# A scan along the adjacency's rows in place of triangle products, in the first layer of a graph network

## The chip, the cores and the metric

The kernel runs on one core of one Trainium2 chip. The metric is the device time of one execution in microseconds (us). The profile is of one execution, taken by the hardware profiler.

The engines are called as the profile calls them: PE multiplies matrices, PEld is its loading of weights, DVE is the vector engine, ACT the scalar engine with its activation functions, POOL the general engine (GpSimd), and SP issues transfers. Each works through a fixed list of instructions in order and waits where an operand isn't ready.

## What is computed

Four graph layers run over 2708 nodes with 512 features, with one adjacency matrix of 2708 x 2708 zeros and ones (int32). Each layer ends with a residual and a layer norm. The change touches layer 0, and the mask that the later layers read:

```
Ab   = A > 0
keep = Ab & (cumsum(Ab, axis=1) <= 64)          # each node's first 64 neighbours
cnt  = keep.sum(axis=1)
xj   = leaky_relu((keep @ X) / max(cnt, 1) @ W_nb.T + b_nb)
xi   = leaky_relu(X @ W_line.T + b_line)
x    = layernorm(X + xi + where(cnt > 0, xj, 0))
# layer 1: mask = A > 0; agg = mask @ x / max(mask.sum(1), 1); ...
# layers 2 and 3: attention over A > 0
```

So layer 0 has to know, for each one in a row of A, whether it is among the first 64 of its row. Layer 1 and the attention layers need the whole mask.

## The kernel before, in words

Rows and columns are cut into NT = 22 tiles of 128 nodes, the last with 20. `maskT` is the transposed mask, kept on the chip for the whole program in 8-bit floats: `maskT[p, j, i]` belongs to neighbour 128 j + p and node i.

**Mask stage of layer 0** (the loop of lines 276 to 296). For each tile t PE makes two products of 512 x 512 weights with the transposed features: `pm0` with W_nb (line 280), which `keep_y` (214) splits into a high part yH (ACT) and a low part yL (DVE)[...]; and `pm1` with W_line (288), to which DVE adds the bias (290) and applies leaky (182), after which POOL adds the residual (292) and stores r0 to memory (293). Beside that `load_mask` (234, POOL's queue) brings 128 rows of A as bf16, `count` (240 to 245, DVE) counts each row's ones and derives four small columns (`iso`, `has`, `rkeep`, `rdeg`), and `turn` (249 to 259) transposes the rows with 22 small PE products into maskT, with ACT copying out. Mask tiles have two buffers `m`. Up to t = 2 the order on PE is written by hand (`pe`); later each engine's list follows from the program's order, its priorities and readiness as the scheduler sees them. `issue_after` lets `count` stand after a given instruction.

**Sums of layer 0** (393 to 421). The node tiles form six blocks (`cuts`): tiles 20 and 21 first, then five blocks of four. For each block the loop goes over the 22 neighbour tiles j; such a pass through the loop is called a step here. Two PE products per step keep a running count of neighbours in `cum` (a buffer of pm0): with `upper`, a triangle of ones, which gives the count down to each row of this tile (311), and with `below`, its complement, which completes the tile's count afterwards (401). DVE compares the running count with 64 and multiplies by the mask, which gives kT (313). kT has two buffers. Four or eight products (408) add kT times yH and yL to one sum per node tile. Beside it two generators step on: `todo`, which finishes the previous block's nodes (`finish`, 321: two steps for each node tile, with the layer norm and the store of x1), and `later`, which multiplies layer 1's weights together (`weights1`, 339) and forms vectors for the attention layers (`vectors`, 370). `later` steps once in block 1, from j = 2 in block 2, and every second time from there.

**Layer 1** makes its products per tile (426 to 436: yH, yL again, and z1), and then its sums (439 to 456), where ACT widens maskT to fp32 (447) and PE multiplies it with yH and yL (450).

The transfer queues: mask loads, r0, x1 and z1 stores are issued by POOL; feature rows, weights and read-backs by SP.

Of the kernel before, what the change touches and what calls it, by code (L numbers as in the profile page):

```python
# [30 lines left out]
def kernel(  # L31
# [43 lines left out]
    rkeep = const.tile([P, NT], F32, name="rkeep")  # L75
    for c, value in ((iso, 0.0), (has, 0.0), (rdeg, 1.0), (rkeep, 1.0)):
        nc.vector.memset(c, value)

    dcol = const.tile([P, NT, H], F32, name="dcol")
    nc.vector.memset(dcol, 0.0)  # L80


# [41 lines left out]

    def transpose_weight(pool, psum, dst, src):

        for ki in range(KD):
            wr = pool.tile([P, D], F32, name="wr", bufs=4)
            nc.sync.dma_start(wr, src[ki * P:(ki + 1) * P, :])
            ps = psum.tile([P, KD, P], F32, name="ps_tr")  # L130
            for ko in range(KD):
                pe(nc.tensor.transpose(ps[:, ko, :], wr[:, ko * P:(ko + 1) * P], ident))
            nc.vector.tensor_copy(dst[:, :, ki * P:(ki + 1) * P], ps)  # L133
# [47 lines left out]
    def leaky(dst, u):  # L181
        nc.vector.scalar_tensor_tensor(dst, u, 0.01, u, op0=OP.mult, op1=OP.max)

# [6 lines left out]
    with ExitStack() as phase:  # L190
        yp = phase.enter_context(tc.tile_pool(name="y", bufs=1))

        upper = yp.tile([P, P], BF16, name="upper")
        make_upper_triangular(nc, upper)
        below = yp.tile([P, P], BF16, name="below")
        nc.vector.tensor_scalar(below, upper, -1.0, 1.0, op0=OP.mult, op1=OP.add)
        weight2 = yp.tile([P, KD, D], F32, name="weight2")
# [20 lines left out]
        def product(xT, n, w, which, order=as_it_comes):  # L218
# [3 lines left out]
            return pm  # L222

        def rows_of(src):
            return early(2, NT, lambda t: fetched(src, t, rows(t)))

        with ExitStack() as ph:
            st = ph.enter_context(tc.tile_pool(name="l0a", bufs=2))
            wnT, wlT = weight(), weight2

            def load_mask(t):
                n = rows(t)
                m = st.tile([P, N], BF16, name="m")
                nc.gpsimd.dma_start(m[:n], adj[t * P:t * P + n, :], max_dma_last_dim=N * 2)
                return m

            def count(t, m):
                n = rows(t)
                cnt = sm.tile([P, 1], F32, name="cnt")
                nc.vector.tensor_scalar(m[:n], m[:n], 0.0, None, op0=OP.is_gt, op1=OP.add, accum_out=cnt[:n])  # L240
                one = slice(t, t + 1)
                nc.vector.tensor_scalar(iso[:n, one], cnt[:n], 0.0, None, op0=OP.is_equal)
                nc.vector.tensor_scalar(has[:n, one], cnt[:n], 0.0, None, op0=OP.is_gt)
                nc.vector.tensor_scalar(rkeep[:n, one], cnt[:n], KEEP, 1.0, op0=OP.min, op1=OP.max)
                nc.vector.tensor_scalar(rdeg[:n, one], cnt[:n], 1.0, None, op0=OP.max)

            def turn(t, m, order=as_it_comes):
                n = rows(t)
                for g0 in range(0, NT, G):
                    g1 = min(g0 + G, NT)  # L250
                    ps = sums(BF16, (P, G, P))
                    for j in range(g0, g1):
                        w = rows(j)
                        order(nc.tensor.transpose(ps[:w, j - g0, :n], m[:n, j * P:j * P + w], identb[:n, :n]))  # L254
                    parts = [(P, g0, min(g1, FULL))] + ([(rows(FULL), FULL, NT)] if g1 > FULL else [])
                    for w, a, b in parts:
                        if a < b:
                            nc.scalar.copy(maskT[:w, a:b, t * P:t * P + n], ps[:w, a - g0:b - g0, :n],
                                           saturate=False)

            xs = rows_of(x)
            xTs = early(0, NT, lambda t, order=as_it_comes: transposed(ahead, ps_tr, xs(t), rows(t), "xT", order))
            ms = {}

            transpose_weight(st, ps_tr, wnT, l0_w_nb)
            lows = {}
            for t in range(2):
                xT = xTs(t, order=pe)  # L270
                lows[t] = keep_y(t, P, product(xT, P, wnT, 0, pe))
            transpose_weight(st, ps_tr, wlT, l0_w_line)
            b_line = bias(bcast(l0_b_line, D))
            for i in range(2):
                ms[i] = load_mask(i)
            for t in range(NT):
                n = rows(t)
                order = pe if t < 3 else as_it_comes
                if t > 1:
                    lows[t] = keep_y(t, n, product(xTs(t), n, wnT, 0, order))  # L280
                xT = xTs(t)
                if t + 1 < NT:
                    xTs(t + 1)
                for q in range(0 if t == 2 else t - 1, t) if t > 1 else ():
                    turn(q, ms[q], order)
                    if q + 2 < NT:
                        ms[q + 2] = load_mask(q + 2)
                pm = product(xT, n, wlT, 1, order)
                u = sm.tile([P, D], F32, name="u")
                nc.vector.tensor_add(u[:n], pm[:n], b_line[:n])  # L290
                leaky(u[:n], u[:n])
                nc.gpsimd.tensor_add(u[:n], u[:n], xs(t))
                nc.gpsimd.dma_start(r0_dram[t * P:t * P + n, :], u[:n])
                with tc.issue_after(lows[t].ins):
                    count(t, ms[t])
            turn(NT - 1, ms[NT - 1])
            nc.vector.reciprocal(rkeep, rkeep)
            nc.vector.reciprocal(rdeg, rdeg)

        with ExitStack() as ph:
            st = ph.enter_context(tc.tile_pool(name="l0b", bufs=1))
            b_nb = bias(bcast(l0_b_nb, D))
            cuts = [(b, min(b + 4, NT)) for b in range(0, NT, 4)]
            cuts = cuts[-1:] + cuts[:-1]

            def kept(cum, b, j):
                cols, w = slice(b[0] * P, b[1] * P), (b[1] - b[0]) * P  # L310
                nc.tensor.matmul(cum[:, :w], upper, maskT[:, j, cols], start=(j == 0), stop=True, skip_group_check=True)  # L311
                kT = st.tile([P, 512], F32R, name="kT", bufs=2)
                nc.vector.scalar_tensor_tensor(kT[:, :w], cum[:, :w], KEEP, maskT[:, j, cols],  # L313
                                               op0=OP.is_le, op1=OP.mult)
                return kT

            def begin(b):
                cum = ps_mm.tile([P, D], F32, name="pm0")
                return cum, kept(cum, b, 0)

            def finish(ts_, us):
                for t in ts_:
                    n, u = rows(t), us[t]
                    r0 = fetched(r0_dram, t, n)
                    nc.vector.tensor_add(u[:n], u[:n], b_nb[:n])
                    leaky(u[:n], u[:n])
                    yield
                    nc.vector.scalar_tensor_tensor(u[:n], u[:n], has[:n, t:t + 1], r0, op0=OP.mult, op1=OP.add)
                    layer_norm(sm, u[:n], n, u[:n])
                    nc.gpsimd.dma_start(x1_dram[t * P:t * P + n, :], u[:n])  # L330
                    yield
# [60 lines left out]

            todo, later = iter(()), chain(weights1(), vectors())
            cum, kT = begin(cuts[0])
            for i, b in enumerate(cuts):
                ts_ = range(*b)
                cols, w = slice(b[0] * P, b[1] * P), (b[1] - b[0]) * P
                pa = {t: sums() for t in ts_}
                for j in range(NT):
                    if j + 1 < NT:  # L400
                        nc.tensor.matmul(cum[:, :w], below, maskT[:, j, cols], start=False, stop=True,  # L401
                                         skip_group_check=True)
                        nxt = kept(cum, b, j + 1)
                    elif i + 1 < len(cuts):
                        cum, nxt = begin(cuts[i + 1])
                    for t in ts_:
# [4 lines left out]
                    next(todo, None)  # L411
                    if i == 1 and j > 1 or i > 1 and j % 2 or i == 0 and j == 2:
                        next(later, None)
                us = {}
# [4 lines left out]
                todo = finish(ts_, us)  # L419
            for _ in later:  # L420
                pass
# [4 lines left out]
            for t in range(NT):  # L426
                n = rows(t)
                xT = xTs(t)
                keep_y(t, n, product(xT, n, wnb[0], 0))
                if t + 1 < NT:  # L430
                    xTs(t + 1)
# [794 lines left out]
```

## Time and profile before

| | us |
|---|---|
| three runs | 3123.17, 3125.3, 3129.33 |
| median | 3125.3 |
| profiled execution, span | 3125.8 |
| its PE busy | 3009.5 (96%) |
| its DVE busy | 1988.8 (64%) |
| its ACT busy | 1401.3 (45%) |

The span falls into the mask stage of layer 0 (to 218 us), the sums of layer 0 (218 to 537), the products of layer 1 (537 to 698), its sums (698 to 924) and the attention layers, over two thirds of the time. A line of a view names the place in the kernel (L408 is line 408), the engine, the operation, and the tile that is written and those that are read (`kT<-pm,maskT`). "Idle before <-" is time in which the engine had nothing to do ahead of these instructions, with what ended it. PE's ends are modelled because products are pipelined, so starts are the better measure: the distance of two starts is what an instruction costs.

### The profile page before, as it was taken

Reading aid. Unit: us, or ns where it says so; the run is one execution under the profiler, and the core shown is the slowest. Engines: PE = TensorE matmul, PEld = TensorE weight load, DVE = VectorE, ACT = ScalarE, POOL = GpSimd, SP = SyncE. Lnnn points to the kernel's source line nnn. Section 1 sums busy time; section 2 is a strip of 40 time slices with the busy share of each in tenths; the row PEclk is TensorE's granted clock in tenths of the full one; section 3 lists DMA queues with packets and bytes.
Section 4 is the critical chain, followed back from the end, with each engine's and each line's share of the span. In section 5 each row is a group of like instructions: output and inputs, shape, how many; then the busy total and the mean of one; then the engine's idle time right before and its main releaser. Section 6 shows DMA issues by size and latency. Waiting matters only on the chain.

```text
span 3125.8 us, 37086 instructions
## 1 busy us (share of the span) xinstructions
PE 3009.5 (96%) x14888; PEld 1647.0 (53%) x14888; DVE 1988.8 (64%) x2562; ACT 1401.3 (45%) x1575; POOL 223.2 (7%) x352
## 2 busy tenths in 40 slices
PE   8999999999999999999998999999999999999998
PEld 4556666448887433333356333333356455555555
DVE  5562765212233899999986999999963524345342
ACT  2431000112224688888863788899863000000011
POOL 2220010101110000000012000000000000000001
PEclk9999999999999999999999999999999999999999
DMA  5651421322222000110024010011021000000000
GB/s 137 139 127 35 121 64 41 108 65 81 81 70 76 15 29 35 39 44 30 28 80 145 22 39 28 27 38 33 20 97 48 4 14 17 24 14 22 14 19 21
DMA packets 114287, 163.31 MB, mean 52 GB/s; under 512 B 39494, under 2 KB 62311, under 8 KB 114104
## 3 DMA queue, kind: packets, MB, share of 16 engines
q1 hardware_dynamic: 88152, 109.21, 11.5%
q0 software_dynamic: 16064, 47.95, 5.6%
q10 hardware_dynamic: 9888, 3.67, 0.5%
q8 instruction: 119, 1.95, 0.3%
q14 instruction: 64, 0.52, 0.1%
HBM read 130.92 MB, written 44.55 MB: 56 GB/s over the span
## 4 chain that ended last, share of the span: by engine, by line
PE 65%; issue 19%; DVE 10%; ACT 2%; DMA 2%; POOL 1%; DVEq 0%; POOLq 0%; SPq 0%; ACTq 0%
PE pn L857 13%; PE pm L221 10%; PE po L734 9%; PE acc L450 7%; DVE e L598 6%; PE acc L408 5%; PE pm L529 5%; PE pl L832 5%; PE pl L823 5%; PE pd L665 2%; ACT c L606 1%; PE ps_tr L120 1%; PE acc L254 1%; DMA rows<-o_dram 1%; PE pm L401 1%
## 5 line engine op out<-in xcount | busy, mean ns | idle before, releaser
L598 DVE SCALAR_TENSOR_TENSOR e<-v_bc,ucol,maskT 128x1300 f32<-128x1300 f32 (+3 forms) x836 | 1187.4, 1473 | 345.6 <-PE pn L857 317.9
L606 ACT ACTIVATE c<-e,bcol 128x1300 fp8e4<-128x1300 f32 (+1 forms) x704 | 993.9, 1423 | 113.0 <-DVE e L598 61.7
L734 PE MATMUL po<-e,R 128*64 128x512 f32 (+2 forms) x4224 | 946.4, 550 | 47.4 <-DVE e L598 47.3
L734 PEld LDWEIGHTS po<-e,R 128*64 128x64 f32 x4224 | 340.5, 136 | 600.3 <-issue 384.9
L857 PE MATMUL pn<-e,R 128*128 128x512 f32 (+1 forms) x1056 | 413.5, 542 | 0.0
L857 PEld LDWEIGHTS pn<-e,R 128*128 128x128 f32 x1056 | 191.0, 190 | 199.4 <-issue 195.9
L529 PE MATMUL pm<-w,xT 128*128 128x264 f32 (+3 forms) x1056 | 247.7, 388 | 17.1 <-ACT xT L122 16.6
L529 PEld LDWEIGHTS pm<-w,xT 128*128 128x128 f32 (+1 forms) x1056 | 191.3, 187 | 58.5 <-ACT xT L122 24.4
L408 PE MATMUL acc<-yH,kT 128*128 128x512 f32 x484 | 214.0, 442 | 0.0
L825 ACT ACTIVATE w<-pl,b 128x256 f32<-128x256 f32 (+1 forms) x88 | 40.9, 465 | 372.9 <-PE pl L823 372.9
L450 PE MATMUL acc<-yH,mf 128*128 128x512 f32 x484 | 192.7, 398 | 0.0
L408 PE MATMUL acc<-yL,kT 128*128 128x512 f32 x484 | 192.4, 398 | 0.0
L450 PE MATMUL acc<-yL,mf 128*128 128x512 f32 x484 | 190.2, 393 | 0.0
L221 PE MATMUL pm<-w,xT 128*128 128x512 f32 (+1 forms) x384 | 175.1, 598 | 2.4 <-ACT xT L122 1.4
L113 POOL TENSOR_TENSOR ln_rs<-ln_rs,half 128x1 f32<-128x1 f32 x88 | 51.6, 586 | 1693.0 <-DVE ln_rs L112 1691.7
L221 PE MATMUL pm<-weight,xT 128*128 128x512 f32 (+1 forms) x352 | 162.3, 604 | 3.6 <-DVE weight L133 2.8
L313 DVE SCALAR_TENSOR_TENSOR kT<-pm,maskT 128x512 fp32r<-128x512 f32 (+1 forms) x132 | 84.8, 642 | 123.6 <-PE pm L311 122.9
L832 PE MATMUL pl<-lin,w 128*128 128x512 f32 (+1 forms) x352 | 157.4, 592 | 0.0
L823 PE MATMUL pl<-lin 128*128 128x256 f32 (+1 forms) x704 | 153.4, 371 | 3.7 <-DVE lin L756 3.7
L823 PEld LDWEIGHTS pl<-lin 128*128 128x128 f32 x704 | 129.1, 190 | 34.5 <-issue 15.8
L447 ACT CAST mf<-maskT 128x1024 fp32r<-128x1024 fp8e4 (+1 forms) x66 | 64.3, 976 | 163.2 <-PE acc L450 160.9
L215 ACT CAST yH<-pm 128x512 fp32r<-128x512 f32 (+1 forms) x44 | 25.7, 585 | 245.7 <-PE pm L221 245.7
(172 smaller groups left out, 2518.3 us busy)
## 6 DMA issues: line engine op xcount, KB each, us to landing
rows<-x_dram SPq DMA_DIRECT2D x63, 256.0 KB
m<-in_adj_dram POOLq DMA_DIRECT2D x21, 677.0 KB, 6.3
v_bc<-v_dram SPq DMA_DIRECT2D x16, 704.0 KB
x_dram<-u POOLq DMA_DIRECT2D x42, 256.0 KB, 2.3
rows<-o_dram SPq DMA_DIRECT2D x42, 256.0 KB
v_bc<-v_dram SPq DMA_DIRECT2D x16, 650.0 KB
o_dram<-o SPq DMA_DIRECT2D x32, 256.0 KB
rows<-in_x_dram SPq DMA_DIRECT2D x21, 256.0 KB
```

Source lines behind the costliest of these rows:

```text
L221: order(nc.tensor.matmul(pm[:n], xT[:, k, :n], w[:, k, :], start=(k == 0), stop=(k == KD - 1)))
L313: nc.vector.scalar_tensor_tensor(kT[:, :w], cum[:, :w], KEEP, maskT[:, j, cols], op0=OP.is_le, op1=OP.mult)
L408: nc.tensor.matmul(pa[t], kT[:, (t - b[0]) * P:(t - b[0] + 1) * P], y[:, j, :], start=(j == 0 and y is yH), stop=(j == NT - 1 and y is yL))
L447: nc.scalar.copy(mf[:, :g1 - g0, :], maskT[:, g0:g1, t * P:(t + 1) * P])
L450: nc.tensor.matmul(pa, mf[:, j - g0, :], y[:, j, :], start=(j == 0 and y is yH), stop=(j == NT - 1 and y is yL))
L529: nc.tensor.matmul(pm[a][:n, :D // 2 + heads], xT[:, k, :n], w[:, k, a, :D // 2 + heads], start=(k == 0), stop=(k == KD - 1))
L598: nc.vector.scalar_tensor_tensor(e[:, :w], v[:, :w], ucol[:, j, h:h + 1], maskT[:, j, c0:c0 + w], op0=OP.max, op1=OP.mult)
L606: nc.scalar.activation(c[:, :w], e[:, :w], AF.Sigmoid, bias=bcol[:, j, h:h + 1], scale=STEP, saturate=False)
L734: pe(nc.tensor.matmul(po[i][HO * k:HO * k + HO, :c1 - c0], R2[:, j, h * HO:(h + 1) * HO], e[:, c0:c1], start=(j == 0), stop=(j == NT - 1)))
L823: nc.tensor.matmul(pl[:, :w], self.lin1[:, k, f * P:(f + 1) * P], h[:, k, :w], start=(k == 0), stop=(k == KD - 1))
L832: nc.tensor.matmul(pl[:n], gT[:, f, (t - t0) * P:(t - t0) * P + n], self.lin2[:, f, :], start=(f == 0), stop=(f == KF - 1))
L857: nc.tensor.matmul(pn[k][:, :w], R2[:, j, k * P:(k + 1) * P], e[:, :w], start=(j == 0), stop=(j == NT - 1))
```

## The change

Three things are done in another way.

Counting moves to the rows of A before they are turned. ACT turns a row tile into ones and zeros with a steep sigmoid and sums each row as it does so (`count`). DVE runs a scan along the row, in two halves (`place`): the state starts at -64.5, each one adds 1, and it is held at 0.5 from above. A product of the mask with the state leaves zero where there is no neighbour, a negative number for the first 64 and 0.5 for all later ones. That is what is turned into maskT, so `kept` needs one comparison (smaller than zero) and no running count. The triangles and their products are gone.

The masks are taken in the order of the blocks (`turns`: tiles 20 and 21, then 0 to 19). The first 18 (HERE) are counted, placed and turned in the mask stage, with three buffers `m`, spread over t = 0 to 18 with a pause at t = 9: the first half after yL, the second after leaky, the turn in the next pass. The other four are handled by `other_masks` beside the sums, in the buffer of the weight `w` and the room of `spare`. `later` starts when these are done, and then steps every time.

Since maskT no longer holds zeros and ones, DVE cleans it with 22 instructions (not equal to zero) before layer 1's sums read it. `has` and `rkeep` are derived later, per tile and per block. The pieces of the layer-0 weights are loaded into parts of maskT that are still unused.

```diff
-        upper = yp.tile([P, P], BF16, name="upper")
-        make_upper_triangular(nc, upper)
-        below = yp.tile([P, P], BF16, name="below")
-        nc.vector.tensor_scalar(below, upper, -1.0, 1.0, op0=OP.mult, op1=OP.add)
...
+        HERE = NT - 4
+        cuts = [(b, min(b + 4, NT)) for b in range(0, NT, 4)]
+        cuts = cuts[-1:] + cuts[:-1]
+        turns = [t for b in cuts for t in range(*b)]
...
+        def count(i, m):
+            t, n = turns[i], rows(turns[i])
+            nc.scalar.activation(m[:n], m[:n], AF.Sigmoid, bias=gate[:n], scale=STEP, accum_out=cnts[:n, t:t + 1])
+
+        def place(i, m, places, half_):
+            n = rows(turns[i])
+            c0, c1 = ((0, N // 2), (N // 2, N))[half_]
+            nc.vector.tensor_tensor_scan(places[:n, c0:c1], m[:n, c0:c1], over[:n].to_broadcast([n, c1 - c0]),
+                                         places[:n, c0 - 1:c0] if half_ else -KEEP - 0.5, OP.add, OP.min)
+            nc.vector.tensor_mul(m[:n, c0:c1], m[:n, c0:c1], places[:n, c0:c1])
...
-                nc.vector.tensor_scalar(m[:n], m[:n], 0.0, None, op0=OP.is_gt, op1=OP.add, accum_out=cnt[:n])
...
-            wr = pool.tile([P, D], F32, name="wr", bufs=4)
+            wr = room[ki]
...
+            room = [maskT[:, G + k, :4 * D].bitcast(F32) for k in range(2 * KD)]
...
+            masks = early(1, HERE, lambda i: load_mask(i, st.tile([P, N], BF16, name="m", bufs=3)))
...
+                now = counted < min(HERE, -(-(t + 1) * HERE // (NT - 2)))
+                if now:
+                    m, places = masks(counted), st.tile([P, N], BF16, name="places", bufs=1)
+                    count(counted, m)
+                    with tc.issue_after(lows[t].ins):
+                        place(counted, m, places, 0)
...
+                if now:
+                    with tc.issue_after(low.ins):
+                        place(counted, m, places, 1)
+                    counted += 1
...
-                nc.tensor.matmul(cum[:, :w], upper, maskT[:, j, cols], start=(j == 0), stop=True, skip_group_check=True)
                 kT = st.tile([P, 512], F32R, name="kT", bufs=2)
-                nc.vector.scalar_tensor_tensor(kT[:, :w], cum[:, :w], KEEP, maskT[:, j, cols],
-                                               op0=OP.is_le, op1=OP.mult)
+                nc.vector.tensor_scalar(kT[:, :w], maskT[:, j, cols], 0.0, None, op0=OP.is_lt)
                 return kT
...
+            def other_masks():
+                places = st.tile([P, KD * D * 2], BF16, name="spare", tag="spare")
+                for i in range(HERE, NT):
+                    m = load_mask(i, ahead.tile([P, 2 * KD * (D + 2 * H)], BF16, name="w", tag="w", bufs=1)[:, :N])
+                    for _ in range(5):
+                        yield
+                    count(i, m)
...
-                        nc.tensor.matmul(cum[:, :w], below, maskT[:, j, cols], start=False, stop=True,
-                                         skip_group_check=True)
-                        nxt = kept(cum, b, j + 1)
+                        nxt = kept(b, j + 1)
...
-                    if i == 1 and j > 1 or i > 1 and j % 2 or i == 0 and j == 2:
-                        next(later, None)
+                    next(chain(first, later) if i else first, None)
...
+                nc.vector.tensor_scalar(maskT[:, t, :], maskT[:, t, :], 0.0, None, op0=OP.not_equal, saturate=False)
```

## The prediction

> **What bounds the kernel now.** I read three views: busy time by stretch, the timeline of the stretches that the change touches, and the groups by shape for prices. The stretches are layer 0's mask stage (43 to 218 us), its sums (218 to 537) and layer 1's products (537 to 698).
>
> ```profile
> 43.00:218.00 175.00, 174.47 (x868) 92.57 (x865) 105.11 (x181) 74.21 (x124) 49.18 (x58) 1.00 0.66 139
> 218.00:537.00 319.00, 314.92 (x1338) 215.51 (x1334) 177.57 (x320) 22.93 (x42) 24.70 (x38) 0.99 0.24 66
> 537.00:698.00 161.00, 160.28 (x434) 72.93 (x432) 41.88 (x69) 25.68 (x47) 16.14 (x30) 1.00 0.26 86
> ```
> Columns: stretch, length, busy us of PE, weight load, DVE, ACT, POOL. PE is busy nearly throughout; DVE for 105, 178 and 42 us. Work taken from PE gains time only while DVE, which receives the new work, keeps up **in each stage**.
>
> PE's timeline in the sums shows the steps of a four-tile block:
>
> ```profile
> 354.45 0.39 PE L401 MATMUL pm<-maskT,below 128*128 128x512 fp8e4 x1
> 354.68 0.38 PE L311 MATMUL pm<-maskT,upper 128*128 128x512 fp8e4 x1
> ...
> 356.77 0.39 PE L401 MATMUL pm<-maskT,below 128*128 128x512 fp8e4 x1
> ```
> A step repeats every 2.32 us. The chain in order of time prices its eight sum products alone, since layer 1 runs the same shape with nothing between:
>
> ```profile
> 698.25 226.07 PE acc L450 x968
> ```
> 226.07/968 = 0.2335 us, so 1.87 us for eight; the two triangle products cost the other 0.45 us.
>
> The mask stage repeats every 8.83 us (mask loads start at 90.99, 99.82, 108.65). Its timeline gives the loop from a turn to the next load:
>
> ```profile
> 98.02 1.49 PE L254 MATMUL acc<-identb,m 128*128 128x128 bf16 x22
> 99.82 0.70 POOL L234 DMA_DIRECT2D m<-in_adj_dram  x1 [1.76 <-PE acc L254]
> ```
> The turn takes 1.49 us; the load is issued 0.3 us after it, and lands a median 6.3 us later (the page's DMA part).
>
> Prices from the groups by shape (count | busy, mean ns):
>
> ```profile
> L290 DVE TENSOR_TENSOR u<-pm,bias 128x512 f32<-128x512 f32 x21 | 14.5, 690 | 22.5 <-issue 14.2 <-PE pm L221 8.3
> L755 DVE TENSOR_SCALAR rows<-rows 128x512 f32<-128x512 f32 x21 | 8.9, 422 | 0.7
> L606 ACT ACTIVATE c<-e,bcol 128x1408 fp8e4<-128x1408 f32 x352 | 513.9, 1469 | 60.8 <-DVE e L598 33.8 <-PE pd L665 2.1 <-DVE rc L712 1.7
> L606 ACT ACTIVATE c<-e,bcol 128x1300 fp8e4<-128x1300 f32 x352 | 480.0, 1378 | 52.2 <-DVE e L598 27.8 <-PE pd L665 2.6 <-DVE rc L712 1.5
> ```
>
> [...]
>
> ```profile
> 219.50 1.45 POOL L292 TENSOR_TENSOR u<-u,rows 20x512 f32<-20x512 f32 x1 [6.64 <-DVE u L182]
> 219.68 1.83 DVE L361 SCALAR_TENSOR_TENSOR u<-w,bc,u 128x512 f32<-128x512 f32 x1
> 221.77 0.73 DVE L361 SCALAR_TENSOR_TENSOR u<-w,bc,u 128x512 f32<-128x512 f32 x1
> ```
> The same DVE instruction takes 1.83 us under POOL's addition and 0.73 without.
>
> **The change, part by part.**
>
> *1. Triangle products removed (PE, on the path).* 110 steps x 0.45 = 49.7; 22 two-tile steps x 0.226 (half) = 5.0; less six `below` products that did not exist anyway, 1.0. **-53.7 us.** kT becomes a one-source comparison on fp8, 0.42 us for 512 columns[...] (as L755; bounds 0.42 and 0.69). DVE does it behind 1.87 us of products; it saves 41 us of DVE work (94 to 53), which alone ends nothing.
>
> *2. New prices.* The scan of 1354 elements is in no trace[...]. Sigmoid with count: L606 rises 0.84 ns per element (91 ns for 108), so 2708 take 2.57 us on ACT; with the count's read-out I take 2.65.
>
> *3. Mask stage, 18 tiles (at t = 0 to 18 without 9).* DVE's list for one tile: yL 0.69, scan 2.98, product 0.86, addition 0.69, leaky 0.69, scan 2.98, product 0.86; 9.75 us, about 9.7 with `has` and small overlaps. It replaces 2.96 + 0.6 of counting. PE needs 8.83, so **DVE passes PE**. A second loop closes through ACT, whose built order is yH, xT, casts, then the sigmoid of a mask two places later, then the next yH: from the end of a tile's last product, 12 transposes 0.9, issue 0.3, landing 6.3, sigmoid 2.65, yH 0.6, about 10.8 us, and two tiles' DVE lists must fit round it: (10.8+9.7)/2 = 10.25. POOL's addition (1.26 us, two SBUF inputs) becomes ready just as the second scan starts; full exclusion makes it 9.7+1.26 = 10.95 per tile, or 11.4 with gaps. Bounds 9.7 and 11.4; I take **10.5**. What queues behind each wait: PE's remaining transposes and the next two products behind the second half's product, ACT's yH behind the sigmoid's load. 16 spacings x 1.67 = 26.7, about 1 for the pair round t = 9, and 2 at the start (0 to 4), where two sigmoids and a table load stand in front of the first yH though counting no longer delays the weight copies. Moved away: four turns, 4 x 1.45 = -5.8. **+24 us** (+8 to +41).
>
> *4. Sums.* PE's work: 318 (218.2 to 536.3) includes some 5 of gaps; less 53.7, plus the four turns 5.8, gives 264. Now DVE. kT has two buffers, so in a four-tile step DVE can spend 1.87-0.42 = 1.45 us on other things, with one step's credit. Following the changed kernel's built DVE list at these prices, DVE's sums per block, kT included, are 19.7, 32.4, 38.6, 37.2, 44.8, 46.8 us against bare products of 20.5 and 5 x 41.1. PE's waits:
> - Block 1, 6 us. The tile for mask 18 is free only after the last product with `w`; landing and sigmoid end 5.8 us into the block and the scan at 8.8, while kT reaches to 4.7; then product and scan stand together (3.84).
> - Block 2, 14 us: two masks and two finishes; in steps 23 to 27 13.6 us stand where 8.7 fit (5), in 30 and 31 3 more, and 6 waiting for loads that start only after the turn before (about 10 us from turn to sigmoid's end).
> - Block 3, 6 us: 13.5 in four steps where 7.3 fit. Block 4, 0: layer 1's weight products give PE 3.43 us more in every other step.
> - Block 5, 13 us: `later` now steps every time, so eight steps carry a finish (1.85), a vector pair (1.38) and kT (0.42), 29.2 against 15.0 and credit 1.5.
> - Block 6, 5 us: 14 cleanings of maskT[...] stand between its kTs: 46.8 against 41.1.
>
> 44 us of waits, so 264+44 = 308 or 309 against 318: **-9 us** (waits of 35 to 60: -19 to +6). Thus most of the 53.7 is given back inside the same stage.
>
> *5. Layer 1's products.* The other 8 cleanings, 13 us, are hidden: DVE has 119 of 161 us free. **+1** (0 to 3) for those in front of the first yL.
>
> *Nothing:* the eight weight pieces have room of their own, so SP loads them no later; layer 1's first weight (1 MB on SP) now waits for `w` until the last mask's turn, some 1 to 2 us within the bounds of the sums; the removed memsets, triangles and small counts lie beside PE; `has`, `iso`, `rdeg` and the reciprocals are 0.15 to 0.3 us beside PE. On POOL's queue r0's addition and store stand behind the mask load that waits for a turn; u has two buffers, so nobody waits for them.
>
> Sum: +24 -9 +1 = +16 on 3125.8, **3142 us**. The other runs are 3123.17, 3125.3 and 3129.33, so the span stands at their median.
>
> **Rivals.**
> *A, faster: the scan runs at full rate.* [...] Then DVE's list is 6.9 us, the loop (10.8+6.9)/2 = 8.9, with POOL's addition 9.5: mask stage 16 x 0.3 - 4 = +1; waits of the sums 33, so 297 against 318, -21; +1. **3107.** In between it decides at about 2.3 us a scan, where -19 and +16 cross zero.
> *B, much slower: POOL's exclusion is paid in full at each tile*[...]: 11.4 per tile, 16 x 2.57+2+2-4 = +41, sums -5, +1: **3163**. For it: the 1.83 us above. Against: DVE's next instruction usually starts within 0.1 us of the last.
> *C, faster or the same: the waits overlap more than I price.* Independent DVE instructions start 0.08 us before the previous one's recorded end; if all slack falls so, 9.7 per tile (+8), waits 36 (-17), +1: **3118**.
> That the change doesn't do what it says is excluded: the built list has no triangle products.
>
> **How the numbers follow.** Forecast (3130 to 3158 on its own) 0.48, A 0.16, B 0.16, C 0.13, other 0.07. 0.2% (6 us) is about what a measurement of this kernel can tell from no change. Faster: A, most of C: 0.27. Same: the low end of the forecast, the rest of C: 0.11. Slower: 0.62. The range reaches from A to B, 3107 to 3163.
>
> **What would show it.** Right: scan rows of about 2.98 us; mask loads 10 to 11 us apart in place of 8.83; PE idle before the second-half transposes, released by DVE's product; steps of 1.87 us in the sums with PE waiting for kT in blocks 1 to 3 and near the start of block 5. Wrong: scans of 1.6 us, or a mask stage that stays at 8.8 us per tile; POOL additions that never lengthen a scan or a product would cut off B.

## The result, and the profile after

The changed kernel takes 3154.35 us (median of four runs, 3153.42 to 3156.64) against 3124.64 us of the kernel before (four runs on the same chip, 3123.17 to 3129.33): a ratio of 1.0094 with a 95% interval of 1.0076 to 1.0111, so it is **slower by about 0.9%**. The forecast was 3142, with a range of 3107 to 3163.

In the two profiled executions (3125.8 and 3151.6 us) PE's timeline gives the stages. Each is counted from the first product of its kind to the first product of the next, layer 1's sums to the start of their last product:

| stage | before | after | difference | predicted |
|---|---|---|---|---|
| start and mask stage, to the first sum product | 220.1 | 270.7 | +50.6 | +24 |
| sums of layer 0 | 317.8 | 300.4 | -17.4 | -9 |
| products of layer 1 | 160.3 | 159.4 | -0.9 | +1 |
| sums of layer 1 | 225.7 | 219.3 | -6.4 | none |

What follows is equal within 0.3 us. The forecast for this execution was 10 us too low, because a mask stage that cost twice the estimate was partly paid for by two stages that gave more.

Busy time by stretch, after (stretch, length, busy us and instructions of PE, weight load, DVE, ACT, POOL, then PE's granted clock and the transfers):

```profile
43.00:270.00 227.00, 192.08 (x789) 96.28 (x790) 186.78 (x154) 102.46 (x140) 93.92 (x57) 0.93 0.42 92
270.00:571.00 301.00, 276.39 (x1165) 206.89 (x1164) 195.86 (x356) 43.43 (x61) 50.26 (x41) 0.97 0.31 83
571.00:730.00 159.00, 159.00 (x432) 72.57 (x431) 52.51 (x78) 26.20 (x48) 22.19 (x31) 1.00 0.25 86
```

In the mask stage PE was busy for 174.5 of 175 us before; now it is idle for 35 of 227. But DVE is idle too, for 40 us. Neither engine's own work fills the stage, which points to a ring in which they wait for each other. The clock column says 0.93 where it said 1.00.

The groups by shape (count | busy, mean ns) answer to the prices:

```profile
L244 DVE TENSOR_TENSOR_SCAN places<-m,places,over 128x1354 bf16<-128x1354 bf16 x17 | 51.5, 3032 | 0.0
L244 DVE TENSOR_TENSOR_SCAN places<-m,over 128x1354 bf16<-128x1354 bf16 x17 | 50.4, 2965 | 0.0
L323 DVE TENSOR_SCALAR kT<-maskT 128x512 fp32r<-128x512 fp8e4 x110 | 46.1, 420 | 65.4 <-PE acc L436 65.3
L246 DVE TENSOR_TENSOR m<-m,places 128x1354 bf16<-128x1354 bf16 x34 | 44.4, 1305 | 1.2
```

Scan and kT of 512 columns cost what was predicted (2.98 and 0.42); that of 256 takes 0.32. The product of mask and places does not: 1305 ns on average, not 860. The timelines of one and a half tiles show why. DVE and POOL:

```profile
152.65 3.03 DVE L244 TENSOR_TENSOR_SCAN places<-m,places,over 128x1354 bf16<-128x1354 bf16 x1
155.71 1.74 DVE L246 TENSOR_TENSOR m<-m,places 128x1354 bf16<-128x1354 bf16 x1
...
160.97 0.87 DVE L246 TENSOR_TENSOR m<-m,places 128x1354 bf16<-128x1354 bf16 x1
163.78 0.69 DVE L305 TENSOR_TENSOR u<-pm,bias 128x512 f32<-128x512 f32 x1 [1.93 <-PE pm L221]
```
```profile
152.82 3.91 POOL L307 TENSOR_TENSOR u<-u,rows 128x512 f32<-128x512 f32 x1 [6.78 <-DVE u L181]
```

POOL's addition starts 0.17 us into the second scan and ends at 156.73, one microsecond after it. It lasts 3.91 us. In the kernel before it took 1.26:

```profile
L292 POOL TENSOR_TENSOR u<-u,rows 128x512 f32<-128x512 f32 x21 | 26.4, 1259 | 113.2 <-DVE u L182 113.2
```

Beside it the second product takes 1.74; the first, with no POOL beside it, 0.87. So the addition takes longer beside the scan, and the product longer beside the addition; why is not shown. And PE:

```profile
157.51 1.08 PE L255 MATMUL acc<-identb,m 128*128 128x128 bf16 x12 [3.49 <-DVE m L246]
158.53 5.16 PE L221 MATMUL pm<-weight,xT 128*128 128x512 f32 x8
...
169.98 0.94 PE L255 MATMUL acc<-identb,m 128*128 128x128 bf16 x12 [1.87 <-DVE has L358]
170.85 3.70 PE L221 MATMUL pm<-weight,xT 128*128 128x512 f32 x8
```

The ring can be read off: second product (DVE), 12 transposes that wait for it (PE), the product with the line weight behind them in PE's list, the addition that waits for that (DVE, 1.93 us idle above), leaky, the second scan of the next tile. Once round, from the scan at 165.11 to that at 175.98, is 10.87 us. Some rounds are longer, because the product with the line weight takes 5.2 to 5.4 us in them and not 3.70 (it is four products of the program, which the profile shows as eight); with the 5.16 above the round is 12.46. Seven of these products are slow in the steady stage. The length of the wait alone doesn't decide which. PE was idle for 3.49 us ahead of the one above and for 2.54 ahead of another, but ahead of the other five for the same 1.87 us as ahead of those that took 3.70. One of the five, and below it the busy times of a fast product and of this one:

```profile
78.28 0.94 PE L255 MATMUL acc<-identb,m 128*128 128x128 bf16 x12 [1.87 <-DVE m L246]
79.15 5.40 PE L221 MATMUL pm<-weight,xT 128*128 128x512 f32 x8
```
```profile
68.30:71.80 3.50, 3.50 (x9) 1.61 (x9) 3.47 (x2) 2.11 (x4) 0.70 (x1) 1.00 0.75 183
79.20:84.30 5.10, 5.10 (x9) 2.15 (x9) 3.70 (x2) 2.04 (x4) 0.70 (x1) 0.67 0.83 180
```

The clock that PE was granted is 1.00 in the fast product and 0.67 in the slow one (0.67 to 0.70 in all seven). In run 8 below, which has the same code in this stage, other rounds are long; what picks them is not shown. Sixteen rounds average 11.67 us where 10.5 was predicted.

### The profile page after: what moved, and what is told of

It is laid out like the page before. It is cut to its first block, busy times and chain, and to the rows that moved or that the text cites. A ratio compares the mean times of both kernels' runs of the same rounds, so it can differ in the third digit from the quotient of the medians.

```text
span 3151.6 us, 36663 instructions
## 1 busy us (share of the span) xinstructions
PE 2973.1 (94%) x14630; PEld 1638.9 (52%) x14630; DVE 2101.5 (67%) x2573; ACT 1461.6 (46%) x1621; POOL 299.4 (10%) x350
## 3 DMA queue, kind: packets, MB, share of 16 engines
q10 hardware_dynamic: 9888, 3.67, 0.5%
## 4 chain that ended last, share of the span: by engine, by line
PE 59%; issue 20%; DVE 14%; DMA 4%; ACT 3%; POOL 1%; DVEq 0%; POOLq 0%; ACTq 0%; SPq 0%
PE pn L886 13%; PE po L763 9%; PE pm L221 8%; PE acc L479 7%; DVE e L627 6%; PE pm L558 5%; PE pl L861 5%; PE acc L436 5%; PE pl L852 5%; DVE places L244 2%; PE pd L694 2%; ACT c L635 1%; DMA m<-in_adj_dram 1%; DVE m L246 1%; DMA rows<-o_dram 1%
## 5 line engine op out<-in xcount | busy, mean ns | idle before, releaser
L558 PE MATMUL pm<-w,xT 128*128 128x264 f32 (+3 forms) x1056 | 249.2, 390 | 16.7 <-ACT xT L121 16.2
L436 PE MATMUL acc<-yH,kT 128*128 128x512 f32 x484 | 202.2, 418 | 22.4 <-DVE kT L323 20.5
L558 PEld LDWEIGHTS pm<-w,xT 128*128 128x128 f32 (+1 forms) x1056 | 192.4, 188 | 58.6 <-ACT xT L121 23.8
L221 PE MATMUL pm<-weight,xT 128*128 128x512 f32 (+1 forms) x352 | 173.9, 640 | 0.2 <-DVE weight L132 0.2
L852 PEld LDWEIGHTS pl<-lin 128*128 128x128 f32 x704 | 129.1, 190 | 34.5 <-issue 15.8
L694 PE MATMUL pd<-c,parts_c 128*12 128x384 fp8e4 (+2 forms) x2816 | 130.9, 307 | 0.0
L221 PEld LDWEIGHTS pm<-w,xT 128*128 128x128 f32 (+1 forms) x384 | 71.9, 188 | 101.0 <-issue 90.9
```

Of the source, the lines that this page charges most:

```text
L221: order(nc.tensor.matmul(pm[:n], xT[:, k, :n], w[:, k, :], start=(k == 0), stop=(k == KD - 1)))
L436: nc.tensor.matmul(pa[t], kT[:, (t - b[0]) * P:(t - b[0] + 1) * P], y[:, j, :], start=(j == 0 and y is yH), stop=(j == NT - 1 and y is yL))
L558: nc.tensor.matmul(pm[a][:n, :D // 2 + heads], xT[:, k, :n], w[:, k, a, :D // 2 + heads], start=(k == 0), stop=(k == KD - 1))
L694: pe(nc.tensor.matmul(p[32 * g:32 * g + 12, :c1 - c0], parts_c[:, j, h, :], c[:, c0:c1], start=(j == 0 and h == hs[0]), stop=(j == NT - 1 ...
L852: nc.tensor.matmul(pl[:, :w], self.lin1[:, k, f * P:(f + 1) * P], h[:, k, :w], start=(k == 0), stop=(k == KD - 1))
```

## The experiments

Every kernel was compared with the kernel before on the same chip; ratios carry their 95% interval. "Mask stage" is the time of the first sum product, 270.7 in the changed kernel and 220.1 before.

**1. An elementwise pass in place of each scan** (the changed kernel):

```diff
-            nc.vector.tensor_tensor_scan(places[:n, c0:c1], m[:n, c0:c1], over[:n].to_broadcast([n, c1 - c0]),
-                                         places[:n, c0 - 1:c0] if half_ else -KEEP - 0.5, OP.add, OP.min)
+            nc.vector.scalar_tensor_tensor(places[:n, c0:c1], m[:n, c0:c1], -KEEP - 0.5,
+                                           over[:n].to_broadcast([n, c1 - c0]), op0=OP.add, op1=OP.min)
```

> In place of both scans of every tile stands one elementwise pass over the same operands (minimum of mask minus 64.5 and 0.5), which carries no count along the row: all 2,708 places hold the same value, so layer 0 keeps no neighbour and the output is another one. The pass should take about 1.6 us in place of 2.97. Theory DVE (the mask stage is as long as VectorE's own work per tile): both passes of a tile count, 2 x 1.4 us x 17 tiles = -47 us in the mask stage, total about 3105. Theory loop (the stage is as long as the ring: product of the second half, 12 transposes, the product with the line weight, addition, leaky, second scan): only the second scan is in the ring, 1.4 x 17 = -24 us, total about 3128; as the ring is then no longer slow enough for the PE to fall idle for over 3 us, the 5.16 us products could go too, a further -12, 3116. The rival of the prediction (a scan at full rate) asked for 3107.

Measured: 3113.14 us, 0.9954 (0.9938 to 0.9971); mask stage 236.3, -34.4; the pass takes 1.56 us. (The expectation has one thing wrong: the value is -63.5 wherever there is a one, so layer 0 keeps all neighbours, not none. The instructions are the same either way.) The gain of the stage lies where the ring says, one scan per tile and the slow rounds (-24 to -36), not where DVE's whole work says (-47): the first scan has slack beside the line product. Most rounds take 9.47 us, 1.40 less than 10.87, which is the saving of one scan and not of two. It also shows what the scan's length costs: with 1.56 us in place of 2.97 to 3.03 the kernel gains on the one before, as rival A said (3107). Rival A's DVE list of 6.9 us is 9.75 with two scans of about 1.56; no run shows a scan so short.

**2. No GpSimd addition:**

```diff
-                nc.gpsimd.tensor_add(u[:n], u[:n], xs(t))
```

> The addition of x on GpSimd is left out, so the rows that layer 0 stores lack their residual x. Theory exclusion (the second product takes 1.74 us and not 0.87 [...]): all second products take 0.87, -0.88 us per tile in the mask stage whoever bounds it, about -15 us; total about 3139. If the PE's wait before the 12 transposes thereby falls from 3.49 to about 2.6 us and its products no longer run slow (5.16 us), another -6 to -12: 3128 to 3133. Rival (the long product has another cause, such as the PE or DMA writing the same memory): products stay at 1.74, 3154.

Measured: 3140.91 us, 1.0044 (1.003 to 1.0059); mask stage 251.1, -19.7. The second products take 0.86 us, 0.88 less, 15 us over the tiles: it is POOL's addition that makes them longer. Of the seven slow products of the steady stage one is left; the rest of the gain goes with them. What the addition costs DVE is 30% of the 50.6 us.

**3. PE kept busy** by two products that nobody reads, ahead of the waiting transposes:

```diff
+                if g0 == G and order_warm:
+                    wp = psum().rearrange("p g c -> p (g c)").bitcast(F32)
+                    for q in range(2):
+                        order(nc.tensor.matmul(wp, ident, weight2[:, q, :], start=True, stop=True))
```

> Two extra 128x512 products of the identity (about 1.8 us together, nobody reads them) stand before the transposes of the second half from the third tile on, where the PE waits 1.9 or 3.5 us. Theory slow restart (the product after an idle PE of over 3 us runs at 5.16 us and not 3.6 to 3.7, and that product is in the ring): all these products take 3.6 to 3.7, the spacing of the mask stage evens out at about 10.9 us, -1.5 us in every second tile = about -12 us; total about 3142. Rival (the long product has another cause than idleness, or it is not on the path): 5.16 stays every second tile, or goes without effect, total 3154; if the extra work delays the transposes, up to +10.

Measured: 3145.8 us, 1.0062 (1.0046 to 1.0079); mask stage 263.4, -7.4. **More work on PE makes the kernel faster.** PE's timeline of one round:

```profile
76.95 1.94 PE L255 MATMUL acc<-weight,ident 128*128 128x512 f32 x4
78.72 1.35 PE L259 MATMUL acc<-identb,m 128*128 128x128 bf16 x14
80.00 3.70 PE L221 MATMUL pm<-weight,xT 128*128 128x512 f32 x8
```

All rounds of about 12.5 us are gone but one beside the pause at t = 9 (12.3), and most take 10.87 to 10.91; of the seven slow products one is left there, at 4.55. So with the fillers on PE six of the seven slow products go, and they are on the path. Two things in the expectation are wrong. It asks for an idle of over 3 us, where 1.87 was enough in five of the seven cases. And not every second round was slow: five rounds were 1.7 us longer for it, 8.5 us together, while the first round and those at the pause (13.6, 21.7 and 12.3) have other waits, which stay.

**4. Products first**, the ring cut by one move in program order:

```diff
+                pm = product(xT, n, wlT, 1, order)
                 while turned < counted:
                     for _ in turn(turned, masks(turned), lambda: sums(BF16, (P, G, P)), order):
                         pass
                     turned += 1
...
-                pm = product(xT, n, wlT, 1, order)
```

> One move: the product with the line weight comes ahead of the transposes of the tile before in program order, everything else as it is. Theory loop: the ring is cut, as VectorE's addition no longer waits for transposes that wait for VectorE; what is left per tile is VectorE's own work, 2 scans 5.95 + 2 products 1.73 to 2.6 + subtraction, addition, leaky 2.1 = 9.8 to 10.6 us in place of 11.7: -18 to -30 us, total 3125 to 3136. Theory DVE (VectorE's own work with its exclusions sets the stage): nothing, 3150 to 3158.

Measured: 3130.76 us, 1.0012 (1.0004 to 1.0021); mask stage 244.7, -26.0, rounds of 10.5 us. PE's timeline:

```profile
176.57 0.94 PE L255 MATMUL acc<-identb,m 128*128 128x128 bf16 x12 [1.20 <-DVE m L246]
177.45 3.70 PE L221 MATMUL pm<-w,xT 128*128 128x512 f32 x8
```

PE still waits for DVE, but what follows the transposes is now the next tile's other product, which DVE doesn't yet need. DVE has no gap left in a round: 10.5 us is its own list, with one product at 1.75. This is the ring shown; nothing else was changed. But the slow products are gone here as well, and most of the gain is not the 0.37 us by which a fast round of the ring (10.87) exceeds DVE's list. From the first scan of a second half to the last such scan 22.8 us are saved: about 10 in the six slow rounds, 5 from 10.87 to 10.5, 3.6 in the first round and 4.3 at the pause. The ring is costly because what delays one engine in it, such as a product slower by 1.7 us, makes the whole round longer by as much.

**5. Residual late**: products first, and x added by DVE in the finishing of the sums in place of POOL in the mask stage.

```diff
-                nc.gpsimd.tensor_add(u[:n], u[:n], xs(t))
...
+                    nc.vector.tensor_add(u[:n], u[:n], x_)
```

> On top of the products-first order, x is no longer added on GpSimd in the mask stage but on VectorE after layer 0's sums (22 additions of 0.69 us there and one more fetch per tile). If both causes of the long mask stage hold and are separate (the ring, and the GpSimd addition that lengthens each second product from 0.87 to 1.75 us), VectorE's work falls from 10.5 to 9.6 us per tile: first product of the sums at about 230 us, -15 from the 244.7 of products-first, sums unchanged to +4 as VectorE has room there; total 3116 to 3121, faster than before. If the two overlap (the same time counted twice), the mask stage stays at 240 to 245, total about 3130. If the additions and fetches hold up the sums, up to +15 there and no gain.

Measured: 3125.74 us, 0.9993 (0.9984 to 1.0001); mask stage 229.0, another -15.8, rounds of 9.62 us. The same group of products as above:

```profile
L246 DVE TENSOR_TENSOR m<-m,places 128x1354 bf16<-128x1354 bf16 x34 | 29.4, 866 | 1.2
```

44.4 - 29.4 = 15.0 us is what POOL's addition cost DVE. With the ring cut, this cost comes on top of the 26.0. But the sums grew from 302.2 to 310.6 us: in block 5 the finishing work, now longer by the additions, stands with the weight vectors ahead of kT, and PE waits there five times for 1.4 to 3.4 us. Half of the gain was given back.

**6 and 7. Places.** The gain in layer 1's sums is in a stage whose instructions the change does not touch: the fast products of a pair (yH, yL) follow each other at 0.2267 us in the changed kernel and 0.2333 before. The first theory was alignment to 64 bytes; an unused tile of 32 bytes at the head of the pool shifts all operands.

```diff
+        nc.vector.memset(yp.tile([P, 8], F32, name="pad"), 0.0)
```

> The kernel before with one unused tile of 32 bytes per partition at the head of the pool that holds yH and yL: everything after it in SBUF moves by 32 bytes, no instruction of the stages changes. In the kernel before yH, yL and the weights stand 32 bytes beyond a multiple of 64, in the kernel after on a multiple of 64. Theory placement (fp32r products of 512 columns follow each other at 0.2267 us where the operands stand on a multiple of 64 bytes, at 0.2333 where not): layer-1 sums 968 products x 0.0066 = -6.4 us (225.7 to 219.3), layer-0 sums as many, -6.4; total about 3112. Rival (the faster products of the kernel after come from its instruction mix or from the chip): 225.7 stays, 3125.

Measured: 3127.07 us, 1.0 (0.9991 to 1.0009); layer 1's sums 225.7. No effect.

> The changed kernel with the same 32 bytes: its operands now stand where those of the kernel before stood, 32 beyond a multiple of 64. Theory placement: layer-1 sums 219.3 to 225.7, layer-0 sums +4 to +6.4 (the steps that wait for VectorE hide some of it), total 3164 to 3168, and the change at equal placement costs about +40 us, not +27. Rival: nothing moves, 3154.

Measured: 3158.37 us, 1.0097 (1.008 to 1.0114); layer 1's sums 219.4. No effect: alignment falls.

**10, 11 and 12. Distance.** The 32 bytes left one thing alone: the distance from the moving operand (yH, yL) to the weights (mf, kT). A gap between the two pools changes it.

```diff
+        for _ in range(2):
+            nc.vector.memset(sm.tile([P, 1], F32, name="cntpad"), 0.0)
```

> Changed kernel with 64 unused bytes between yL and the pools that hold kT and mf. In the kernel before and with 32 bytes at the head the distance from yH to mf is 106,816 bytes, an odd multiple of 64, in the changed kernels 106,752, an even one; here it is made odd. Theory distance (fp32r products go at 0.2267 us where weights and moving operand stand an even multiple of 64 bytes apart, 0.2333 where odd): layer-1 sums 219.3 to 225.7, layer-0 sums +4 to +6; total about 3165. Rival (the speed does not come from places in SBUF): 219.3 stays, 3154.

Measured: 3165.88 us, 1.0116 (1.0101 to 1.0132); layer 1's sums 225.7, layer 0's 304.3 (+3.9). The changed kernel loses its unexplained gain by 64 unused bytes. The chain in order of time has the whole stage as one piece:

```profile
736.44 226.08 PE acc L482 x968
```

> The kernel before with the same 64 bytes between yL and the later pools: distance from yH to mf 106,880, an even multiple of 64. Theory distance: layer-1 sums 225.7 to 219.3, layer-0 sums 317.8 to about 311; total about 3112 to 3115. Rival: 225.7 and 3125 stay.

Measured: 3125.99 us, 0.9995 (0.9988 to 1.0001); layer 1's sums 224.8. So "even multiple of 64" was wrong as a rule. The last run took the distance 256 bytes beyond a multiple of 512, as in the changed kernel, with tiles of 224 bytes in place of 4.

> The kernel before with 448 unused bytes between yL and the later pools: the distance from yH to mf becomes 107,264 bytes, 256 beyond a multiple of 512, as in the changed kernel (106,752), where the two slow distances seen so far are 320 and 384 beyond one. Theory distance modulo 512: layer-1 sums 225.7 to 219.3, layer-0 sums 317.8 to about 311.5, total about 3113; at equal placement the change then costs about 40 us and not 29. Rival (only this one distance is fast, or the sums before are held by their triangles anyway): 224 to 226 in layer 1, total 3125; or layer 1 alone gains, total 3119.

Measured: 3118.34 us, 0.9976 (0.9968 to 0.9983); layer 1's sums 219.3, layer 0's 315.2 (-2.6).

```profile
693.29 219.66 PE acc L453 x968
```

| yH to mf, bytes | beyond a multiple of 512 | kernels | layer 1's sums, us |
|---|---|---|---|
| 106,752 | 256 | after, 7 | 219.3, 219.4 |
| 107,264 | 256 | 12 | 219.3 |
| 106,816 | 320 | before, 6, 10 | 225.7 |
| 106,880 | 384 | 11 | 224.8 |

In these seven kernels the speed goes with the distance modulo 512: kernels with the same remainder agree though their operands stand at different places. The place of the weights alone is not strictly excluded. Modulo 512, mf stands at 288, 448 and 480 where layer 1's sums take 219.3 us and at 0, 352, 384 and 416 where they take 225, so a rule of place would need two separate ranges for the shorter time. Only three remainders of the distance were tried, and why it matters stays open. The kernel before gains 7.5 us from 448 unused bytes alone. Against that kernel the change costs about 36 us (3154.4 - 3118.3, or 37 by the two ratios, as they ran on different chips).

**8. Fillers spread** (the changed kernel; the first remaining mask counted 12 steps after its load, the others 6, and a step between product and reduction of the weight vectors):

```diff
-                    for _ in range(5):
+                    for _ in range(12 if i == HERE else 6):
                         yield
                     count(i, m)
...
                     nc.vector.tensor_mul(wr, wr, ab)
+                    yield
```

> Changed kernel, with the fillers of the sums spread: the first remaining mask is counted 12 steps after its load and not 5, the others 6, and each weight-vector step is cut in two steps (product, reduction). Theory lateness (the PE's waits of 4.6, 1.7, 1.5 and 4.2 us in the first two blocks come from VectorE and ScalarE standing behind a mask that has not landed, those of 3.0 and 2.3 in block 5 from vector work of 1.4 us on top of the finishing work in one step): about 10 us of the waits in blocks 6 and 1 go, with the slow products after them, and 4 of block 5; sums 300 to about 288, total 3140 to 3144. Rival (VectorE's total work in those blocks sets the waits, spreading only moves them): sums 297 to 301, total 3151 to 3155.

Measured: 3147.3 us, 1.0068 (1.0051 to 1.0085); sums 294.2, -6.2, about half of what was expected. (What the expectations of runs 8 and 9 call blocks 6 and 1 are the first two in order.) Block 5's waits of over 1 us went, while block 3 got one of 4.9 us in place of 1.9, so some only moved. The first did not go: it is still 4.57 us at 10 us into the sums. In DVE's built list the first scan stands behind the same five kTs as in the changed kernel, so the scheduler sets its place, not the step. It comes to the head of DVE's list at 272.6 and waits there for the count until 275.9, with the next kT behind it.

**9. All together**: residual late, each remaining scan held behind the kT of its step, waits of 12 and 6 steps as above, and the weight vectors moved beside layer 1's products.

```diff
-                        place(i, m, places, half_)
+                        with tc.issue_after(kept_last[0].ins):
+                            place(i, m, places, half_)
...
+                next(last_, None)
```

> Residual-late kernel, whose sums took 310.6 us with 24 us of waits, with the fillers of the sums re-placed: each remaining scan is issued after the kT of its step (so that VectorE does not stand at a scan whose mask has not been counted, with kT behind it), the first mask is counted 12 steps after its load and the others 6, and the 24 weight-vector steps run beside layer 1's products, where VectorE is busy for a third of the time. Theory (the waits are a matter of what stands ahead of kT on VectorE): the waits of 4.4 and 4.0 us in blocks 6 and 1 fall to about 1.5 each, those of block 5 (2.5, 2.0, 3.4, 1.4) go, the slow products after them too; sums 310.6 to 288-294, layer-1 products unchanged within 3; total 3106 to 3112, faster than both. Rival (VectorE's total work bounds those blocks): sums 300 to 308, total 3117 to 3125.

Measured: 3102.15 us, 0.9912 (0.9899 to 0.9926): **faster than both**, by 25 us than the kernel before and by 52 than the changed one (57 by the two ratios, as that ran on another chip). It is also a little faster than expected. Its mask stage and sums:

```profile
43.00:228.00 185.00, 177.96 (x766) 87.43 (x767) 168.43 (x154) 102.95 (x139) 22.64 (x36) 1.00 0.48 108
228.00:516.00 288.00, 271.22 (x1158) 202.37 (x1157) 185.36 (x346) 43.36 (x61) 31.37 (x40) 0.98 0.33 90
```

The first sum product comes at 227.6 (-43), the sums take 288.9 (-11.5), layer 1's products 162.6 (+3.2, the weight vectors). PE is idle for 7 us of the mask stage in place of 35, and its clock is at 1.00. Part of the gain over the kernel before is the distance: against run 12, which has it too, 16 us remain (20 by the two ratios; the runs were on different chips).

## Why the prediction was right, and where it was off

*Triangle products removed:* right. *Prices:* right to 0.1 us, as far as they are an instruction's own time; the sigmoid takes 2.55 + 0.19 and not 2.65. No view of the kernel before shows the scan's 2.98, its product's 0.86 or the 13 us for eight cleanings. The changed kernel has 2.97 to 3.03 for a scan, 0.87 for a product without POOL beside it, and 1.62 for a cleaning:

```profile
L458 DVE TENSOR_SCALAR maskT<-maskT 128x2816 fp8e4<-128x2816 fp8e4 x22 | 35.3, 1618 | 0.0
```

*Mask stage, +24: mis-sized, the term T = 10.5 us per tile.* DVE's own list was predicted at 9.7, and run 5 shows 9.62 when nothing else binds. To that come two terms. POOL's addition was seen and put between nothing and its own 1.26 (an estimate, with one DVE instruction of 1.83 us in place of 0.73 to go by); it is 0.88 on each second product (runs 2 and 5). With it DVE's list is 10.5 (run 4), which is T itself. The other was missed: the text names what queues behind the second half's product, PE's transposes and the next two products, but does not follow on to who waits for the first of these. It is DVE's addition, and so the ring closes. The second loop that was found, through ACT, gave 10.25 and was not the one that bound. A fast round of the ring is 10.87; what makes the average 11.67 are the slow products, which stand inside the ring and were not priced. No view of the kernel before could show them in its steady stage, since PE was never idle there, but its start has products as long: the first with W_nb took 5.61 us (at 11.99), the second 3.67. A common cause was not shown: the clock column has 1.00 over that first one. So 16 rounds at 11.67 for 10.5 make 18.7 us, the pair round the pause at t = 9 took 21.5 and not 18.7, and the first product with the line weight came 4.5 us late (29.27 to 33.73) and not 2: 24 of the 26.6 us. B, POOL's addition paid at each tile, came true in that each second product is longer beside it, but by 0.88 and not as the whole of the gap; even its 11.4 was too short.

*Sums, 264 + 44.* The waits are where they were put, block by block (predicted 6, 14, 6, 0, 13, 5; in the trace 4.6, 7.9, 4.0, 0, 6.4, 1.4), at half the size: about 24 us. But products after a wait are slow here too:

```profile
280.56 0.50 PE L436 MATMUL acc<-yH,kT 128*128 128x512 f32 x1 [4.60 <-DVE kT L323]
...
281.68 0.63 PE L436 MATMUL acc<-yL,kT 128*128 128x512 f32 x1
282.10 0.63 PE L436 MATMUL acc<-yH,kT 128*128 128x512 f32 x1
```

They start 0.43 us apart. Over the stage 88 products start 0.3 to 0.7 us apart, 16.6 us more than at 0.227. Waits and slow products make 41 us. That this is close to the 44 is luck: the waits were priced at nearly twice their size, and the slow products not at all. Of the 8 us by which the stage is shorter than forecast, 3 are this difference and 3.9 the distance (run 10); the rest is not accounted for. (The forecast's sum has a slip of 1 us: 318 less 5, less 53.7, plus 5.8 is 265, not 264.)

*Layer 1's products:* as forecast, within 2 us. *Layer 1's sums:* there was no term; the new pools moved the operands, and that was worth 6.4 us (taken away in run 10, and given to the kernel before in run 12).

The likeliest case was the right one in direction and in its main steps: DVE passes PE in the mask stage and most of the triangle products' 53.7 us is given back in the sums. What sets the length of a round was not in it. That the total is only 10 us off is partly luck, as two errors of opposite sign stand behind it: the mask stage was 26.6 too short, the other stages 16.7 too long, and about 10 of these come from the distance (6.4 and 3.9), for which the prediction has no term.

## What to carry to other kernels

When an engine's new work makes it a partner in step with another, add up the ring, not only each engine's list: follow each wait to who waits for what is queued behind it, until it closes or ends. Here one line moved in program order cut it, for 26 us. And before a gain or loss in an untouched stage is argued with, look where its operands stand: here 64 unused bytes cost layer 1's sums 6.4 us (run 10).

## What the runs showed of the hardware

- In the mask stage four fp32 products behind the transposes took 5.2 to 5.4 us in place of 3.7 in seven rounds of the changed kernel, with a granted clock of 0.67 to 0.70, where a product of 3.7 had 1.00. PE had been idle for 1.87 us ahead of five of them, 2.54 and 3.49 ahead of the others; ahead of most that took 3.7 it had been idle for 1.87 too. In runs 1, 2, 4 and 5, where PE waited less per round, only one steady product took so long (beside the pause in run 2, after 4.2 us idle), and with useless products to keep PE busy only one did as well (run 3, 4.55 us). In the sums fp32r products started 0.43 us apart in place of 0.23 for some 3 us after a wait of 4.6 us, with a granted clock of 0.56, and 1.00 in the 5 us after that.
- fp32r products of 512 columns follow each other at 0.2267 us on average in some kernels and 0.2333 in others, and in the seven compared here this goes with the distance of moving operand and weights in SBUF (table above). In the kernel before the starts are uneven, 0.237 after a yH product and 0.230 after yL; in the changed kernel both are 0.227. With all operands moved by 32 bytes (run 6) the stage took the same 225.7 us.
- POOL's addition of two SBUF operands, 1.26 us in the kernel before, lasted 3.9 us beside a scan of 3.0, and then stretched DVE's next product from 0.87 to 1.75; beside an elementwise pass of 1.56 (run 1) it lasted 2.5, and the product took 1.8.
- The scan of 1354 bf16 elements takes 2.97 to 3.03 us, and an elementwise pass over the same operands 1.56 (run 1).
